# Shift products of two heads in their own row quarters of the TensorE array

## The chip, the cores and the metric

The kernel runs on one core of one Trainium2 chip. The metric is the device time of one execution in microseconds; the median of three executions of the kernel before is 4314.11 us (4312.82 to 4318.57).

The engines of a core have their own in-order instruction streams and meet through semaphores. TensorE multiplies (the profile calls its matmuls PE and its weight loads PEld), VectorE is DVE, ScalarE is ACT, GpSimd is POOL, and SyncE, or SP, issues the DMA transfers.

## What is computed

A transformer block with attention and a feed-forward network side by side on the same normalised input, in float32. The input has 8 sequences of 1024 tokens with 512 features; there are 16 heads of 32 features, and the network is 1408 wide.

```python
xn = _layernorm(x, axis=-1)
x = x + attention(xn) + ffn(xn)

# attention
qkv = xn @ W_attn + b_attn                     # q, k, v: 16 heads of 32
att = einsum('bhqd,bhkd->bhqk', q, k) * 32 ** -0.5
att = where(causal, att, -inf)
att = softmax(att, axis=-1)
y = einsum('bhqk,bhkd->bhqd', att, v)          # heads joined again
y @ W_proj + b_proj

# ffn: fp4_linear quantises and dequantises both operands in blocks of 16
h = silu(fp4_linear(xn, w_gate)) * fp4_linear(xn, w_up)
fp4_linear(h, w_down)
```

## The kernel before

**Streams.** One Python generator writes each kind of work: the projections to q, k and v (`prepare`, L464 and L509), the row maxima and sums of the scores (`maxima`, L594 to L608), the attention itself (`weigh`), the network (`network`, L793 and L815), its quantisation, and the output projection (`finish`, L920). `merge` interleaves them by hand into one program order. It keeps a planned clock: each `yield` names the TensorE cost of what was just issued, the time before which the next step should not begin, and how many banks that step wants. Actions for the other engines are put on a list with due times (`Later`) and come into the program when the planned clock passes them. So a cost in a `yield` does no work on the chip; it decides the order in which the streams are put.

**Banks.** Six PSUM banks of 128 x 512 (`Banks`) are shared by all streams. `take` hands out the one that should be free first, `back` returns it with the time at which its last reader should be done. Two more banks hold `y` and `acc`.

**A unit** is two heads (HU = 2) of one sequence; there are 64 units, eight for each sequence. A softmax here takes two passes. `maxima` finds each query's maximum, which is turned and kept in DRAM as a shift, split into a rounded part and a remainder. `weigh` then computes the scores again with keys on the partitions and queries along the columns, lays the shift onto them, and takes the exponential.

**The shift product.** `shT` is a 128 x 512 tile in F32R that is zero but for the first two rows of each quarter of 32 rows: quarter k = 2Q + r holds the two parts of the shift of head r for the half Q of the queries. `pick` holds four 128 x 128 matrices; the k-th is one in the rows of quarter k and zero elsewhere. The product of `pick[:, k, :]` with `shT` therefore adds up quarter k's rows, and puts the same sum on all 128 output partitions. It opens the accumulation in a bank; the score product (L713, keys as weights, queries as moving operand) closes it.

**The loop of `weigh`.** For each half Q of 512 queries, `j` runs over the key tiles of 128 keys that the causal mask lets through: 4 for Q = 0, 8 for Q = 1. On the diagonal only the columns from `q0` on are computed, so blocks are 512, 384, 256 or 128 columns wide. A block does, for each of the two heads in turn: take a bank, shift product (L710), score product (L713), exponential on ScalarE (L721), and on the diagonal a triangular select on GpSimd (L727). Per unit that is 12 blocks, 24 shift products and 24 score products; over all units 768 blocks.

After every second block `weighted` multiplies four such results with the values (L692). These four products have 32 output rows each and are placed side by side in the columns of the array by `tile_position=(0, row)`; each is a float32 product of two instructions, so a group has eight. There are 384 groups. Everything else on TensorE uses the array undivided.

The shift and score products are F32R and take one instruction each. The projections, the network and the weighting are float32, and take two.

Of the kernel before, what the change touches and what calls it, by code (L numbers as in the profile page):

```python
# [27 lines left out]
def kernel(  # L28
# [35 lines left out]
    HD = D // HEADS  # L64
# [6 lines left out]
    HU = 2  # L71
# [3 lines left out]
    W = QG * P  # L75
# [38 lines left out]
    pick = const.tile([P, HPC, P], F32R, name="pick")  # L114
# [33 lines left out]
    def act(columns, after=0.0, function="other"):  # L148
        if function == "other":
            function = table[0]  # L150
        switch = TABLE if function != table[0] else 0.0
        table[0] = function
        return on("act", 0.17 + 0.00083 * columns + switch, after)
# [4 lines left out]
    def pool(us, after=0.0):  # L158
        return on("pool", us, after)
# [52 lines left out]
    banks = Banks()  # L212
# [320 lines left out]
    def load_half(un, h):  # L533
        f, r0 = un.u * HU // HPC, un.u * HU % HPC
        for name, pool, s, pieces, lst in (("qs", p5, 0, (0, 0, 1, 1), un.qs), ("ks", p6, 1, (0, 1, 0, 1), un.ks)):
            tl = pool.tile([P, HU, W], F32R, name=name)
            for g, piece in enumerate(pieces):
                nc.sync.dma_start(
                    out=tl.bitcast(F32)[g * HD : (g + 1) * HD],
                    in_=un.batch.qk[s, piece, f, r0 * HD : (r0 + HU) * HD, h * W : (h + 1) * W].rearrange(  # L540
                        "(r d) t -> d r t", d=HD
                    ),
                )
            lst.append(tl)

    def load_values(un):
        for h in range(2):
            v = p4.tile([P, QG, HU * HD], F32, name="vs")
            cols = slice(un.u * HU * HD, (un.u + 1) * HU * HD)
            nc.sync.dma_start(  # L550
                out=v, in_=un.batch.v[h * QG : (h + 1) * QG, :, cols].rearrange("t p e -> p t e")
            )
            un.vs.append(v)
# [114 lines left out]
    def weigh(un):  # L668
        f, r0 = un.u * HU // HPC, un.u * HU % HPC
        emptied = 0.0  # L670
        while un.shT is None:
            yield 0.0, clock[0] + 0.5, 0
        units_begun[0] = un.n

        def loads(Q):
            if un.n + 2 < N:
                load_half(units[un.n + 2], Q)
            if un.n + 1 < N and Q == 0:
                load_values(units[un.n + 1])

        yield 0.0, un.ready, 2

        for Q in range(2):
            Later(1.0, lambda Q=Q: loads(Q))
            y = ps_a.tile([P, W], F32, name="y")
            last = (Q + 1) * QG - 1
            waiting = []
            def weighted():
                for j, r, pr, q0 in waiting:
                    h, jj = j // QG, j % QG  # L690
                    row = (j % 2 * HU + r) * HD
                    nc.tensor.matmul(  # L692
                        y[row : row + HD, q0:],
                        lhsT=un.vs[h][:, jj, r * HD : (r + 1) * HD],
                        rhs=pr[:, q0:],
                        start=(j < 2),
                        stop=(j >= last - 1),
                        skip_group_check=True,
                        tile_position=(0, row),
                    )  # L700
                return 0.3 + (W - min(q0 for _, _, _, q0 in waiting)) * 0.0017

            ready = 0.0
            for j in range(last + 1):
                h, jj = j // QG, j % QG
                q0 = jj * P if h == Q else 0
                fresh = []
                for r in range(HU):
                    bank, w = banks.take()
                    nc.tensor.matmul(  # L710
                        w[:, q0:], lhsT=pick[:, Q * HU + r, :], rhs=un.shT[:, q0:], start=True, stop=False
                    )
                    nc.tensor.matmul(  # L713
                        w[:, q0:],
                        lhsT=un.ks[h][:, r, jj * P : (jj + 1) * P],
                        rhs=un.qs[Q][:, r, q0:],
                        start=False,
                        stop=True,
                    )
                    pr = p8.tile([P, W], F32, name="pr")  # L720
                    nc.scalar.activation(pr[:, q0:], w[:, q0:], AF.Exp)  # L721
                    cost = max(0.22, (W - q0) * 0.00089)
                    end = act(W - q0, clock[0] + cost * (r + 1), "exp")
                    banks.back(bank, end)
                    if h == Q:

                        nc.gpsimd.affine_select(  # L727
                            out=pr[:, q0 : q0 + P],
                            in_=pr[:, q0 : q0 + P],
                            compare_op=ALU.is_ge,  # L730
                            fill=0.0,
                            base=0,
                            pattern=[[1, P]],
                            channel_multiplier=-1,
                        )
                        end = pool(0.37, end)
                    if j == 1 and q0 > 0:

                        nc.gpsimd.memset(pr[:, :q0], 0.0)
                        end = pool(0.2)  # L740
                    fresh.append((j, r, pr, 0 if j < 2 else q0))
                if j % 2 == 0 and waiting:
                    yield 2 * cost, max(ready, emptied), 0
                    yield weighted(), 0.0, 2
                    waiting = []
                else:
                    yield 2 * cost, 0.0, 2 if j < last else 0
                waiting += fresh
                ready = end
            yield 0.0, max(ready, emptied), 0  # L750
            cost = weighted()
            yu = p1.tile([P, W], F32, name="yu")
            nc.scalar.copy(yu, y)
            emptied = act(W, clock[0] + cost)

            def store(Q=Q, yu=yu):
                rows = slice(r0 * HD, (r0 + HU) * HD)
                for part in range(2):
                    nc.sync.dma_start(
                        out=un.batch.y[part, f, rows, Q * W : (Q + 1) * W],  # L760
                        in_=yu[part * HU * HD : (part + 1) * HU * HD, :],
                    )
                un.batch.units_done += Q

            Later(emptied - clock[0] + 0.5, store)
            yield cost, 0.0, 2
# [275 lines left out]
    with tc.manual_schedule(  # L1042
# [10 lines left out]
        for k in range(2 * NC):  # L1053
            w = p8.tile([P, NC, P], F32, name="pr")
# [9 lines left out]
        for col in range(2 * D, 3 * D, 2 * P):  # L1064
            w = p2.tile([P, NC, 2 * P], F32, name="wa")
# [48 lines left out]
        def preparations():  # L1114
            for n in range(AHEAD, N, QT):
# [3 lines left out]
        merge(  # L1119
            [  # L1120
                Stream((weigh(un), 17.5, un.n, 1.0) for un in units),
                Stream((maxima(un), 6.0, un.n - 1 - SOONER, 1.0) for un in units[1:]),
                Stream(networks()),
# [43 lines left out]
```

## Time and profile before

| | |
|---|---|
| median of three executions | 4314.11 us |
| the profiled execution | 4316.67 us |
| its span, first to last instruction | 4315.0 us |
| mean granted TensorE clock | 0.99 |
| shift products, L710 | 1536, 643.7 us busy, 427 ns on average |
| score products, L713 | 1536, 519.4 us busy, 346 ns on average |
| weighting, L692 | 3072 instructions, 358.1 us busy, 509 ns on average |
| exponential, L721 | 1536, 666.9 us busy, 494 ns on average |
| start of the first and of the last shift product | 295.4 and 4192.1 us |

A group's busy time is the time in which at least one of its instructions ran. A matmul's duration goes from its start to the end of its last result, and successive matmuls overlap; so durations add up to more than the span, and what a matmul costs the engine is the distance to the start of the next. Weight loads run in a row of their own beside the matmuls.

### The profile page before, as it was taken

The page shows a single profiled execution, that of the slowest core. Times are in us where ns is not written, and L with a number is a line of the kernel's source. Part 1 is how long each engine was busy: PE and PEld are TensorE (multiplying, and loading weights), DVE is VectorE, ACT ScalarE, POOL GpSimd, SP SyncE. Part 2 cuts the span into 40 slices and gives each one's busy share as a digit, 9 for nine tenths or more (in the row PEclk, how much of TensorE's full clock was granted, in tenths as well). Part 3 has the DMA queues.
Part 4 walks back from the last instruction along what each step waited for, and adds up shares of the span by engine and source line. Part 5 has one row for each costly group of instructions (what it writes and reads, how often), then busy time and mean ns, then how long its engine had stood idle before and what let it go on. Part 6 is the DMA issues. An engine that isn't in the chain of part 4 may idle for free.

```text
span 4315.0 us, 58501 instructions
## 1 busy us (share of the span) xinstructions
PE 4186.5 (97%) x17684; PEld 2574.7 (60%) x17684; DVE 2946.8 (68%) x6811; ACT 2331.1 (54%) x5918; POOL 551.6 (13%) x1295
## 2 busy tenths in 40 slices
PE   7779999999999999999999999999999999999998
PEld 6655556566666666666666666666666555555555
DVE  6786666666666766666766666766666677777755
ACT  2246565655555555555555555555555566666640
POOL 0001111111111111111111111111111111111110
PEclk9889999999999999999999999999999999999999
DMA  5654343454545554555554555554554433433424
GB/s 183 176 165 118 106 118 111 125 153 139 148 141 144 153 159 139 149 140 145 152 159 137 150 140 143 154 160 135 152 138 125 120 84 91 102 85 94 103 57 124
DMA packets 564185, 573.83 MB, mean 133 GB/s; under 512 B 114976, under 2 KB 420128, under 8 KB 563872
## 3 DMA queue, kind: packets, MB, share of 16 engines
q1 hardware_dynamic: 563872, 570.10, 47.8%
q8 instruction: 142, 2.33, 0.2%
q14 instruction: 171, 1.40, 0.1%
HBM read 400.56 MB, written 169.35 MB: 132 GB/s over the span
## 4 chain that ended last, share of the span: by engine, by line
PE 83%; DMA 3%; ACT 2%; DVE 2%; issue 1%; SPq 1%; ACTq 0%; POOL 0%; DVEq 0%
PE bank L815 26%; PE acc L793 13%; PE y L692 7%; PE bank L464 7%; PE bank L710 7%; PE bank L713 6%; PE bank L594 5%; PE bank L920 5%; PE bank L509 4%; PE bank L349 2%; ACT bank L566 2%; DVE neg L608 1%; DMA yT<-y_kept 1%; DMA ks<-y_kept 1%; DMA vs<-v_kept 0%
## 5 line engine op out<-in xcount | busy, mean ns | idle before, releaser
L608 DVE TENSOR_REDUCE neg<-bank 128x1 f32<-128x512 f32 (+3 forms) x1280 | 805.6, 635 | 292.3 <-PE bank L594 265.7
L721 ACT ACTIVATE pr<-bank 128x512 f32<-128x512 f32 (+3 forms) x1536 | 666.9, 494 | 517.5 <-PE bank L713 508.5
L566 ACT ACTIVATE bank<-bank,neg 128x512 f32<-128x512 f32 (+3 forms) x1536 | 857.9, 560 | 113.5 <-DVE neg L608 101.5
L727 POOL TENSOR_SCALAR_AFFINE_SELECT pr<-pr 128x128 f32<-128x128 f32 x1024 | 395.3, 397 | 3145.9 <-ACT pr L721 3139.2
L815 PE MATMUL bank<-wuT,xqT 128*128 128x512 f32 (+1 forms) x1536 | 674.7, 564 | 9.0 <-ACT bank L566 6.5
L815 PE MATMUL bank<-wgT,xqT 128*128 128x512 f32 (+1 forms) x1536 | 671.5, 561 | 0.0
L793 PE MATMUL acc<-wdT,hqT 128*128 128x512 f32 x1408 | 662.9, 595 | 1.3 <-ACT hqT L350 1.3
L594 PE MATMUL bank<-ks,qs 128*128 128x512 f32 (+3 forms) x1536 | 631.1, 469 | 20.1 <-ACT bank L566 14.5
L710 PE MATMUL bank<-shT,pick 128*128 128x512 f32 (+3 forms) x1536 | 643.7, 427 | 5.2 <-DMA shT<-shift_kept 3.6
L713 PE MATMUL bank<-qs,ks 128*128 128x512 f32 (+3 forms) x1536 | 519.4, 346 | 0.0
L606 DVE TENSOR_TENSOR bank<-bank,mask 128x128 f32<-128x128 f32 (+1 forms) x768 | 259.5, 338 | 342.6 <-PE bank L594 253.8
L594 PEld LDWEIGHTS bank<-ks,qs 128*128 128x128 f32 x1536 | 273.2, 191 | 266.4 <-issue 132.6
L476 ACT ACTIVATE full<-bank,bqk 128x256 f32<-128x256 f32 x256 | 107.5, 471 | 572.0 <-PE bank L464 503.6
L710 PEld LDWEIGHTS bank<-shT,pick 128*128 128x128 f32 x1536 | 290.8, 189 | 201.0 <-issue 94.1
L815 PEld LDWEIGHTS bank<-wuT,xqT 128*128 128x128 f32 x1536 | 273.8, 190 | 218.3 <-issue 140.6
L815 PEld LDWEIGHTS bank<-wgT,xqT 128*128 128x128 f32 x1536 | 276.0, 190 | 213.0 <-issue 164.8
L793 PEld LDWEIGHTS acc<-wdT,hqT 128*128 128x128 f32 x1408 | 258.3, 190 | 224.4 <-issue 204.1
L692 PE MATMUL y<-pr,vs 128*32 128x512 f32 (+3 forms) x3072 | 358.1, 509 | 4.7 <-POOL pr L727 4.6
L464 PE MATMUL bank<-xnT,wa 128*128 128x256 f32 x1536 | 352.2, 383 | 0.5 <-ACT xnT L350 0.5
L713 PEld LDWEIGHTS bank<-qs,ks 128*128 128x128 f32 x1536 | 291.2, 190 | 84.4 <-issue 51.9
L464 PEld LDWEIGHTS bank<-xnT,wa 128*128 128x128 f32 x1536 | 292.2, 192 | 64.8 <-issue 27.5
L566 ACT ACTIVATION_READ_ACCUMULATOR bank<-bank,neg 128x1 f32 x1536 | 316.0, 206 | 0.0
(97 smaller groups left out, 4501.5 us busy)
## 6 DMA issues: line engine op xcount, KB each, us to landing
wa<-in_L_attn_W_attn_dram SPq DMA_DIRECT2D x146, 512.0 KB
qs<-qk_kept SPq DMA_DIRECT2D x512, 128.0 KB
ks<-qk_kept SPq DMA_DIRECT2D x512, 128.0 KB
wp<-in_L_attn_W_proj_dram SPq DMA_DIRECT2D x81, 512.0 KB
qk_kept<-high SPq DMA_DIRECT2D x128, 256.0 KB
qk_kept<-full SPq DMA_DIRECT2D x128, 256.0 KB
y_kept<-yu SPq DMA_DIRECT2D x256, 128.0 KB
yT<-y_kept SPq DMA_DIRECT2D x112, 256.0 KB
```

The lines of the kernel that those rows point to most:

```text
L464: nc.tensor.matmul(pq[:, j, :], lhsT=halves[j][:, c, :], rhs=xnT[:, c, :], start=(c == 0), stop=(c == NC - 1),)
L566: nc.scalar.activation(part, part, AF.Exp, bias=neg[:, kind, k + j : k + j + 1], accum_out=sums[:, kind, k + j : k + j + 1],)
L594: nc.tensor.matmul(sc[:, j * n : (j + 1) * n], lhsT=un.qs[Q][:, r, i * P : (i + 1) * P], rhs=un.ks[h][:, r, :n], start=True, stop=True,)
L606: nc.vector.tensor_tensor(corner, corner, mask.unsqueeze(1).broadcast_to([P, count, P]), ALU.add)
L608: nc.vector.tensor_reduce(neg[:, kind, k : k + count], each, AX.X, ALU.max, negate=True)
L692: nc.tensor.matmul(y[row : row + HD, q0:], lhsT=un.vs[h][:, jj, r * HD : (r + 1) * HD], rhs=pr[:, q0:], start=(j < 2), stop=(j >= last - 1 ...
L710: nc.tensor.matmul(w[:, q0:], lhsT=pick[:, Q * HU + r, :], rhs=un.shT[:, q0:], start=True, stop=False)
L713: nc.tensor.matmul(w[:, q0:], lhsT=un.ks[h][:, r, jj * P : (jj + 1) * P], rhs=un.qs[Q][:, r, q0:], start=False, stop=True,)
L721: nc.scalar.activation(pr[:, q0:], w[:, q0:], AF.Exp)
L727: nc.gpsimd.affine_select(out=pr[:, q0 : q0 + P], in_=pr[:, q0 : q0 + P], compare_op=ALU.is_ge, fill=0.0, base=0, pattern=[[1, P]], channe ...
L793: nc.tensor.matmul(tl.acc, lhsT=job.hqT[:, j, :], rhs=wdT[:, i, :], start=(i == 0), stop=(i == NI - 1))
L815: nc.tensor.matmul(job.g, lhsT=job.tl.xqT[:, c, :], rhs=wT[:, c, job.i0 : job.i0 + job.w], start=(c == 0), stop=(c == NC - 1),)
```

## The change

In each block both banks are taken first. Then both shift products are issued, then, for each head, the score product, the exponential and what follows. A shift product now uses only its own quarter: 32 rows of `pick`, 32 rows of `shT`, and the 32 rows of the array from k x 32 on, with all 128 output columns. What it adds up is the same, since the other rows of that `pick` are zero. The score products still use all 128 rows. The planned cost of one head is changed from max(0.22, 0.00089 n) to max(0.2, 0.05 + 0.00067 n) for n columns.

```diff
-                for r in range(HU):
-                    bank, w = banks.take()
+                held = [banks.take() for _ in range(HU)]
+                for r, (_, w) in enumerate(held):
+                    k = Q * HU + r
+                    quarter = slice(k * HD, (k + 1) * HD)
                     nc.tensor.matmul(
-                        w[:, q0:], lhsT=pick[:, Q * HU + r, :], rhs=un.shT[:, q0:], start=True, stop=False
+                        w[:, q0:],
+                        lhsT=pick[quarter, k, :],
+                        rhs=un.shT[quarter, q0:],
+                        start=True,
+                        stop=False,
+                        tile_position=(k * HD, 0),
                     )
+                for r, (bank, w) in enumerate(held):
                     nc.tensor.matmul(
                         w[:, q0:],
                         lhsT=un.ks[h][:, r, jj * P : (jj + 1) * P],
...
                     nc.scalar.activation(pr[:, q0:], w[:, q0:], AF.Exp)
-                    cost = max(0.22, (W - q0) * 0.00089)
+                    cost = max(0.2, 0.05 + (W - q0) * 0.00067)
                     end = act(W - q0, clock[0] + cost * (r + 1), "exp")
                     banks.back(bank, end)
```

## The prediction, made before the result was known

> **What bounds the kernel now.** I read the page's busy shares first, then the busy time by stretch, then the chain of work that ended last, and last the single instructions of TensorE around one block of attention.
>
> ```profile
> span 4315.0 us, 58501 instructions
> ## 1 busy us (share of the span) xinstructions
> PE 4186.5 (97%) x17684; PEld 2574.7 (60%) x17684; DVE 2946.8 (68%) x6811; ACT 2331.1 (54%) x5918; POOL 551.6 (13%) x1295
> ...
> ## 4 chain that ended last, share of the span: by engine, by line
> PE 83%; DMA 3%; ACT 2%; DVE 2%; issue 1%; SPq 1%; ACTq 0%; POOL 0%; DVEq 0%
> PE bank L815 26%; PE acc L793 13%; PE y L692 7%; PE bank L464 7%; PE bank L710 7%; PE bank L713 6%; PE bank L594 5%; PE bank L920 5%; PE bank L509 4%; PE bank L349 2%; ACT bank L566 2%; DVE neg L608 1%; DMA yT<-y_kept 1%; DMA ks<-y_kept 1%; DMA vs<-v_kept 0%
> ```
>
> TensorE is the bound: 97% busy, 83% of the chain, and by stretch 994.5, 993.7 and 991.4 us busy in the three stretches of 1000 us from 1000 to 4000 us. VectorE is busy 68 to 71% there, ScalarE 56 to 60%. So a nanosecond that TensorE gains or loses in a block of attention is nearly a nanosecond of the span. The edited product is L710, 7% of the chain (about 300 us); its partner, the score product L713, has 6%.
>
> The groups with shapes kept apart give the counts (name, form, count, then busy us, mean ns and idle before):
>
> ```profile
> L710 PE MATMUL bank<-shT,pick 128*128 128x512 f32 x768 | 365.8, 476 | 4.6 <-DMA shT<-shift_kept 3.6 <-ACT bank L566 0.8 <-ACT full L476 0.2
> L710 PE MATMUL bank<-shT,pick 128*128 128x384 f32 x256 | 120.4, 470 | 0.3 <-ACT bank L566 0.3
> L710 PE MATMUL bank<-shT,pick 128*128 128x256 f32 x256 | 93.0, 385 | 0.1
> L710 PE MATMUL bank<-shT,pick 128*128 128x128 f32 x256 | 64.4, 277 | 0.2
> ```
>
> The means hold latency that overlaps the next product. What a product costs is the distance to the next start: from a score product to the following shift product the trace has a median of 231 ns at 512 columns, 174 at 384, 118 at 256 and 112 at 128 (the last is held by the weight load, not by the columns).
>
> **The key row: what a change of tiling costs here.** No product is tiled by rows before, but L692 is tiled by columns (four products of 32 columns side by side), so the trace shows what going into and out of a tiled form costs. First the timeline of TensorE's matmuls around one such group, then of its weight loads (start us, duration us, engine, line):
>
> ```profile
> 2017.35 0.39 PE L710 MATMUL bank<-shT,pick 128*128 128x512 f32 x1
> 2017.58 0.40 PE L713 MATMUL bank<-qs,ks 128*128 128x512 f32 x1
> 2017.91 1.06 PE L692 MATMUL y<-pr,vs 128*32 128x512 f32 x8
> 2018.90 0.50 PE L710 MATMUL bank<-shT,pick 128*128 128x512 f32 x1
> 2019.24 0.40 PE L713 MATMUL bank<-qs,ks 128*128 128x512 f32 x1
> ```
> ```profile
> 2017.36 0.19 PEld L713 LDWEIGHTS bank<-qs,ks 128*128 128x128 f32 x1
> 2017.91 0.16 PEld L692 LDWEIGHTS y<-pr,vs 128*32 128x32 f32 x8 [0.36 <-PE bank L713]
> 2018.90 0.19 PEld L710 LDWEIGHTS bank<-shT,pick 128*128 128x128 f32 x1 [0.84 <-issue]
> 2019.01 0.19 PEld L713 LDWEIGHTS bank<-qs,ks 128*128 128x128 f32 x1
> ```
>
> Three things are to be seen. Between full products the weights of the next load while the last one streams (2017.36, under the product of 2017.35). At the border they do not: the load of L692 starts at 2017.91, 0.33 us after the product of 2017.58 began, which streams for 0.23. Over the 384 groups of L692 this is steady: 522 ns from a 512-column f32 product (429 ns in a row of its own kind) to the group, 309 from a 256-column one (216), and out again 522 and 309. So **93 ns of drain in each direction**. Last, the load then has nothing to hide behind. The first L710 after the group lasts 0.50 instead of 0.39, and 0.34 us pass to the next start instead of 0.23. Loads of 32 columns take a median of 109 ns and of 128 columns 188, so 79 ns for 96 columns, about 0.83 ns each: **107 ns exposed for 128 columns**. Into a tiled form with loads of 128 columns and out again, that makes 93+107+93+107 = 400 ns. Inside, the tiled instructions start 7 ns apart (the eight loads of the fence fit in 0.16 us).
>
> **The change, part by part.**
>
> *Removed:* of each block's two shift products one disappears under the other. There are 768 blocks: 384 of 512 columns, 128 each of 384, 256 and 128. 384 x 0.231 + 128 x (0.174 + 0.118 + 0.112) = 88.7 + 51.7 = **140.4 us**. The two products name different rows, different weights and different banks, and L692 shows four column tiles really side by side (four two-instruction products in 0.99 us, where one alone needs 0.86).
>
> *Added:* each block now goes from the full array to row quarters and back, ahead of L713. The trace has no row tiling. Its bounds: below, no drain and hidden loads (7 ns for the second start); above, L692's price, 407 ns with that start. I take the upper end, the nearest row. 768 x 0.407 = **312.6 us**. Two corrections follow. At 128 columns the shift product behind its exposed load streams in 56 ns instead of the load-held 112: -7.2 us. And 121 of the 384 groups of L692 are followed directly by L710: their exit is paid already, and a change from column tiles to row tiles costs one border, not two: 121 x 0.200 = -24.2 us. Sum: 312.6 - 140.4 - 7.2 - 24.2 = **+140.8 us**.
>
> *A rule weighed.* The Trainium skill, "TensorE: Matmul & The Clock Gate", Part 3, gives tiles in one pack a span of one matmul plus about 4 ns for each further tile; by it alone each block drops a product, and the sum is about -137 us. But that describes the inside of a pack. The same skill's "TensorEngine Tiling (Array Packing)", Key Properties, says that changing the tiling mode, as against the tile, drains TensorE. The 93 ns above is that drain seen here for columns; that it is as large for rows no run here shows yet. The first page also says a load of 32 rows by 128 columns takes as long as one of 128 by 128, which is why I put 107 ns, not a quarter, at the entry. A pack of two products is small against two borders: **break-even is 140.4/768 = 183 ns a block**, less than one full border of 200 ns.
>
> *Moved:* both banks are taken ahead of the first product, so the second head's bank is wanted one score product (about 0.23 us) earlier. A block is only begun when the plan sees two banks free, and L710 has 5.2 us of idle ahead of it on TensorE in all: nothing. The two score products now end 0.23 us apart instead of 0.46, while an exponential (L721) takes 0.49 on average; the second head's waits behind the first's, some 0.2 us. The weighted product that needs it is held back by one further block, and its waits on ScalarE and GpSimd are about 36 us in all: nothing again. With that cover gone it would be up to 0.2 us in each of 384 groups, 77 us.
>
> *The plan's cost* for a pair falls from 0.911 to 0.786 us at 512 columns, so the hand-made order will think TensorE further on than it is. This changes which stream goes next and no work. Every instruction and DMA stays; SP's queue keeps its transfers, at slightly other places.
>
> *How much reaches the end.* TensorE has 20 us idle in the 3000 us from 1000 to 4000, but the chain also has 2% ScalarE and 2% VectorE, mostly banks not yet free from L566 and L608; slower blocks give those engines more time. I let a tenth of the 140.8 be absorbed: +127. Against the profiled execution's 4316.67 us (span 4315.0 and 1.67 around it) this is 4444; that execution lies 2.6 above the median 4314.11, so **4441 us** on the median's footing, own range 4395 to 4490.
>
> **Rivals.**
>
> *Row quarters drain little (faster).* Place: the two borders of each block. If a quarter's weights load behind the running full product and only one drain is left, the price is 100 ns: 768 x (0.100 - 0.183) = -64, 4250 us. With nothing left it is 4314 - 135 = about 4180. It decides from under 183 ns a block. For it: the weights of a row tile enter only their own rows, and full products do preload. Against it: L692's weights also have columns of their own and still waited, in every group.
>
> *One border is free (slightly slower or same).* One direction costs 200, the other nothing, or both drain with hidden loads (186): 768 x (0.193 to 0.207 - 0.183) = +8 to +18 us, 4322 to 4332; between this and the forecast lie shorter drains. For it: a 32-row product may leave the array earlier than a 128-row one. Against: L692 shows the same 93 in both directions.
>
> *The quarters do not run side by side.* Then nothing is removed and both borders stay: 141 + 140 = about +280, 4590 us. For it: each streams 128 columns of output into its own bank, which L692's tiles do not. Little else speaks for it.
>
> **How the numbers follow.** Forecast 0.60; one border free or shorter drains, up to 4395, 0.14; faster 0.20, of which 0.08 lies above 4250; not side by side 0.06. The range 4250 to 4500 leaves out 0.12 below, 0.06 above. About 0.2% (9 us) is what a measurement can tell from no change: faster 0.20, same 0.05, slower 0.75.
>
> **What would show it.** In the changed trace: the two L710 of a block start about 7 ns apart, with loads under no product; L710 after a 512-column f32 product starts 522 ns after it, not 429; the first L713 of a block starts about 93 ns later than its predecessor's streaming ends and lasts about 0.50, not 0.40; the second keeps 0.40. If L710's loads begin under the product before, the entry is free and I am wrong there; if L713's first load lies under L710, the exit is. If the two L710 start a product's length apart, the pack does not work.

## The result, and the profile after

The changed kernel takes 4453.69 us (median of four runs, 4449.51 to 4456.17) against 4314.2 us: 1.0319 times as long, 95% interval 1.0302 to 1.0335 (the two medians alone give 1.0323). That is **139.5 us slower**. The forecast was 4441 us, slower, with 4395 to 4490 as its own range. A slower result was right, and so was its cause; three terms of the sum were off and partly offset each other.

The page of the changed kernel, in the parts shown for the kernel before (L712 is now the shift product, L721 the score product, L729 the exponential, L801 and L823 the network):

```profile
span 4454.5 us, 58656 instructions
## 1 busy us (share of the span) xinstructions
PE 4329.3 (97%) x17684; PEld 2439.8 (55%) x17684; DVE 2948.9 (66%) x6811; ACT 2326.0 (52%) x5918; POOL 566.4 (13%) x1295
...
## 4 chain that ended last, share of the span: by engine, by line
PE 88%; ACT 2%; DVE 1%; DMA 1%; issue 1%; SPq 0%; ACTq 0%; POOL 0%; DVEq 0%
PE bank L823 28%; PE acc L801 13%; PE bank L721 9%; PE y L692 7%; PE bank L464 7%; PE bank L712 6%; PE bank L594 6%; PE bank L928 4%; PE bank L509 4%; PE bank L349 3%; ACT bank L566 1%; DMA qs<-inv_kept 0%; DVE neg L608 0%; ACT full L520 0%; ACT pr L729 0%
```

The count of matmuls is the same, VectorE and ScalarE are as busy as before, and TensorE has taken up the whole difference: 4329.3 us against 4186.5. The busy time of the shift products falls, as it should when two run at once (643.7 to 347.8 us). Yet the path hardly gains there (7 to 6%), and the score products on it grow from 6 to 9%, although nothing in them was edited. They carry the way back to the undivided array.

Two blocks of 512 columns in the changed trace, first the timeline of the matmuls and then that of the weight loads (start us, duration us, engine, line):

```profile
2008.95 0.63 PE L692 MATMUL y<-pr,vs 128*32 128x256 f32 x8
2009.50 0.50 PE L712 MATMUL bank<-shT,pick 32*128 32x512 f32 x2
2009.93 0.72 PE L721 MATMUL bank<-qs,ks 128*128 128x512 f32 x2
2010.49 0.40 PE L594 MATMUL bank<-ks,qs 128*128 128x512 f32 x1
2010.82 0.50 PE L712 MATMUL bank<-shT,pick 32*128 32x512 f32 x2
2011.25 0.73 PE L721 MATMUL bank<-qs,ks 128*128 128x512 f32 x2
```
```profile
2009.50 0.18 PEld L712 LDWEIGHTS bank<-shT,pick 32*128 32x128 f32 x2 [0.40 <-issue]
2009.93 0.30 PEld L721 LDWEIGHTS bank<-qs,ks 128*128 128x128 f32 x2 [0.24 <-issue]
2010.27 0.19 PEld L594 LDWEIGHTS bank<-ks,qs 128*128 128x128 f32 x1
2010.82 0.18 PEld L712 LDWEIGHTS bank<-shT,pick 32*128 32x128 f32 x2 [0.36 <-DVE high L489]
```

The two shift products are one row of 0.50 us, so they do lie side by side. From the full product at 2010.49 to the pair it is 0.33 us, where 0.23 would be streaming; the load at 2010.82 starts with its product and not ahead of it, unlike the load of L594 at 2010.27, which lies under the score product. From the pair to the first score product it is 0.43 us, which is 107 ns of load, 0.23 of streaming and 93 ns of drain.

Medians of the distances between starts over the 768 blocks of the changed trace. The row of the drain is 522 less 429 ns, and the step to an undivided product is put at its value before, since it differs by at most 2 ns:

| | 512 columns | 384 | 256 | 128 |
|---|---|---|---|---|
| first to second shift product | 3 ns | 3 | 3 | 3 |
| second shift product to first score product | 427 | 368 | 310 | 253 |
| first to second score product | 337 | 280 | 223 | 163.5 |
| second score product to an undivided product | 231 | 174 | 118 | 112 |
| drain at the entry | 93 | 93 | 93 | 93 |
| sum | 1091 | 918 | 747 | 624.5 |
| four products before | 924 | 696 | 472 | 448 |
| **more** | **167** | **222** | **275** | **176.5** |

With 384 blocks of the first width and 128 of each other that is 64.1 + 86.2 = 150.3 us. In the new order 165 weighting groups, not 121, are followed directly by shift products, and each such place saves one border of 0.2 us (its exit is paid already by the group): 150.3 - 33.0 = **117.3 us**. The other 22 of the 139.5 us are not borders. The experiments were made to find them, and to test the price of a border where it was not fitted.

### The profile page after: what moved, and what is told of

Same layout as the page of the kernel before. It is cut to its first block, busy times and chain, and to the rows that moved or that the text cites. A ratio compares the mean times of both kernels' runs of the same rounds, so it can differ in the third digit from the quotient of the medians.

```text
span 4454.5 us, 58656 instructions
## 1 busy us (share of the span) xinstructions
PE 4329.3 (97%) x17684; PEld 2439.8 (55%) x17684; DVE 2948.9 (66%) x6811; ACT 2326.0 (52%) x5918; POOL 566.4 (13%) x1295
## 4 chain that ended last, share of the span: by engine, by line
PE 88%; ACT 2%; DVE 1%; DMA 1%; issue 1%; SPq 0%; ACTq 0%; POOL 0%; DVEq 0%
PE bank L823 28%; PE acc L801 13%; PE bank L721 9%; PE y L692 7%; PE bank L464 7%; PE bank L712 6%; PE bank L594 6%; PE bank L928 4%; PE bank L509 4%; PE bank L349 3%; ACT bank L566 1%; DMA qs<-inv_kept 0%; DVE neg L608 0%; ACT full L520 0%; ACT pr L729 0%
## 5 line engine op out<-in xcount | busy, mean ns | idle before, releaser
L729 ACT ACTIVATE pr<-bank 128x512 f32<-128x512 f32 (+3 forms) x1536 | 664.4, 490 | 722.2 <-PE bank L721 711.4
L735 POOL TENSOR_SCALAR_AFFINE_SELECT pr<-pr 128x128 f32<-128x128 f32 x1024 | 406.4, 407 | 3322.5 <-ACT pr L729 3312.4
L823 PE MATMUL bank<-wuT,xqT 128*128 128x512 f32 (+1 forms) x1536 | 684.4, 570 | 10.7 <-ACT bank L566 5.2
L823 PE MATMUL bank<-wgT,xqT 128*128 128x512 f32 (+1 forms) x1536 | 672.5, 562 | 0.0
L801 PE MATMUL acc<-wdT,hqT 128*128 128x512 f32 x1408 | 668.4, 599 | 1.3 <-ACT hqT L350 1.3
L594 PE MATMUL bank<-ks,qs 128*128 128x512 f32 (+3 forms) x1536 | 630.2, 472 | 20.9 <-ACT bank L566 18.2
L721 PE MATMUL bank<-qs,ks 128*128 128x512 f32 (+3 forms) x1536 | 483.6, 396 | 0.0
L823 PEld LDWEIGHTS bank<-wuT,xqT 128*128 128x128 f32 x1536 | 277.2, 191 | 259.5 <-issue 180.4
L594 PEld LDWEIGHTS bank<-ks,qs 128*128 128x128 f32 x1536 | 274.8, 191 | 238.3 <-issue 125.0
L823 PEld LDWEIGHTS bank<-wgT,xqT 128*128 128x128 f32 x1536 | 275.1, 190 | 213.0 <-issue 139.0
L801 PEld LDWEIGHTS acc<-wdT,hqT 128*128 128x128 f32 x1408 | 255.3, 190 | 230.4 <-issue 218.1
L712 PEld LDWEIGHTS bank<-shT,pick 32*128 32x128 f32 x1536 | 145.2, 182 | 420.3 <-issue 221.4
L692 PE MATMUL y<-pr,vs 128*32 128x512 f32 (+3 forms) x3072 | 359.1, 511 | 4.0 <-POOL pr L735 3.9
L712 PE MATMUL bank<-shT,pick 32*128 32x512 f32 (+3 forms) x1536 | 347.8, 439 | 2.3 <-ACT xqT L350 1.7
L721 PEld LDWEIGHTS bank<-qs,ks 128*128 128x128 f32 x1536 | 229.8, 189 | 144.7 <-issue 119.0
```

The lines of the kernel that those rows point to most:

```text
L594: nc.tensor.matmul(sc[:, j * n : (j + 1) * n], lhsT=un.qs[Q][:, r, i * P : (i + 1) * P], rhs=un.ks[h][:, r, :n], start=True, stop=True,)
L692: nc.tensor.matmul(y[row : row + HD, q0:], lhsT=un.vs[h][:, jj, r * HD : (r + 1) * HD], rhs=pr[:, q0:], start=(j < 2), stop=(j >= last - 1 ...
L712: nc.tensor.matmul(w[:, q0:], lhsT=pick[quarter, k, :], rhs=un.shT[quarter, q0:], start=True, stop=False, tile_position=(k * HD, 0),)
L721: nc.tensor.matmul(w[:, q0:], lhsT=un.ks[h][:, r, jj * P : (jj + 1) * P], rhs=un.qs[Q][:, r, q0:], start=False, stop=True,)
L735: nc.gpsimd.affine_select(out=pr[:, q0 : q0 + P], in_=pr[:, q0 : q0 + P], compare_op=ALU.is_ge, fill=0.0, base=0, pattern=[[1, P]], channe ...
L801: nc.tensor.matmul(tl.acc, lhsT=job.hqT[:, j, :], rhs=wdT[:, i, :], start=(i == 0), stop=(i == NI - 1))
```

## The experiments

All are compared with the kernel before on the same chip.

| run | median us | against before, us | ratio, 95% interval |
|---|---|---|---|
| e1_plan_only | 4323.60 | +6.7 | 1.0015, 1.0008 to 1.0023 |
| e2_old_cost | 4445.92 | +129.0 | 1.0298, 1.0282 to 1.0313 |
| e3_true_cost | 4452.88 | +135.9 | 1.0313, 1.0297 to 1.0328 |
| e4_order_only | 4320.15 | +3.2 | 1.0005, 0.9997 to 1.0014 |
| e5_one_by_one | 4872.11 | +557.1 | 1.1290, 1.1274 to 1.1307 |
| e6_pack_of_four | 4365.90 | +50.9 | 1.0117, 1.0102 to 1.0132 |
| e7_shift_in_score | 4184.69 | -130.3 | 0.9697, 0.9680 to 0.9713 |
| e8_total_17 | 4170.31 | -144.1 | 0.9668, 0.9651 to 0.9684 |
| e9_total_10 | 4133.09 | -181.4 | 0.9579, 0.9565 to 0.9594 |

### The plan alone, and the tiling under other plans

e1 is the kernel before with the new planned cost:

```diff
-                    cost = max(0.22, (W - q0) * 0.00089)
+                    cost = max(0.2, 0.05 + (W - q0) * 0.00067)
```

> The kernel before, with the new planned cost alone: no row tiling, shift and score products in the old order within a block. Theory A (the borders of the row tiling are the whole loss): within 10 us of before, 4304 to 4324 us. Theory B (the plan's clock, which runs ahead of TensorE, costs about 20 us by worse interleaving): 4330 to 4340 us.

It is 6.7 us slower (3.5 to 10 by the interval), just inside A's window and below B's: by itself the plan costs little, but not nothing.

e2 is the changed kernel with the line with the minus, and e3 the changed kernel with

```diff
-                    cost = max(0.2, 0.05 + (W - q0) * 0.00067)
+                    cost = max(0.31, 0.2 + (W - q0) * 0.00067)
```

> The changed kernel with the old planned cost. From the changed trace, a block costs 167, 222, 275 and 177 ns more at 512, 384, 256 and 128 columns, 150 us over all blocks, less 0.2 us for each weighting group that is followed directly by shift products. Theory A: 4425 to 4455 us, like the changed kernel within 15 us. Theory B: some 20 us under the changed kernel, 4430 to 4436 us.

> The changed kernel with a planned cost that fits what its trace shows (0.2 us + 0.00067 us a column for one head, at least 0.31). Theory A: within 15 us of the changed kernel's 4454. Theory B: the loss over the bare border sum (117 us) goes, 4430 to 4436 us.

Both windows of e2 hold its 4445.9; e3 is in A's and not in B's. But the traces say more than the times, because the plan also decides how often a weighting group and a pair of shift products share a border. The steps of a block are the same to 1 ns in the traces of e2 and e3, so the border sum can be made for each:

| | shared borders | 150.3 less 0.2 each | measured | left over |
|---|---|---|---|---|
| changed kernel | 165 | 117.3 | 139.5 | 22 |
| e2, old planned cost | 121 | 126.1 | 129.0 | 3 |
| e3, planned cost as measured | 73 | 135.7 | 135.9 | 0 |

The intervals of the ratios make each left-over uncertain by about 7 us. So the rest of 22 us goes with the new planned cost, the one that runs furthest ahead of TensorE. B had the size right. It missed e3 because the truthful plan puts 92 fewer groups beside shift products and so pays 18 us more in borders. Of the 22, e1 shows 7 without any tiling; the other 15 appear only with tiling and this plan together.

In the middle of the kernel, where the order repeats from unit to unit, borders alone fit. Between the 384th and the 960th score product a unit takes 64.78 us before and 66.82 in e2: +2.04, where 150.3/64 less 1.5 shared borders of 0.2 is 2.05. The changed kernel takes 66.53 there, +1.74, and its border sum, with 2.5 shared borders a unit, is 1.85. So its 22 us lie outside the middle, and most of them ahead of it: at the 384th score product it is 47.5 us behind the kernel before, where borders make 29.6 (16 units of 2.35, less 40 shared borders). In that stretch its clock is lower. The clock rows of the two pages, in 40 slices of the span and in tenths, and the granted clock over the whole span, each first before and then changed:

```profile
PEclk9889999999999999999999999999999999999999
PEclk9888999999999999999999999999999999999999
core 0: 4315.0 us, clock 0.990
core 0: 4454.5 us, clock 0.986
```

One less the granted share, times the span, is the clock lost: 43 us before, 62 in the changed kernel, 56 in e1, 53 in e2 and in e3. In none of the five is any lost between the 384th and the 960th score product. The 19 us more of the changed kernel have about the size and the place of what is left over, so the new plan seems to cost time through the clock. No run shows that as the cause; e2 and e3 also lose 10 us of clock more than the kernel before, with next to nothing left over.

### The order alone

e4 issues both shift products and then both score products, all on the undivided array and with the old planned cost (cut from its difference to the changed kernel):

```diff
                     nc.tensor.matmul(
                         w[:, q0:],
-                        lhsT=pick[quarter, k, :],
-                        rhs=un.shT[quarter, q0:],
+                        lhsT=pick[:, k, :],
+                        rhs=un.shT[:, q0:],
                         start=True,
                         stop=False,
-                        tile_position=(k * HD, 0),
                     )
```

> Both shift products first and then both score products, as in the changed kernel, but all on the undivided array and with the old planned cost. Theory A (order costs nothing): 4309 to 4319 us, score and shift products 231 ns apart as before. Theory C (the two exponentials of a block come too close together, and the second bank is wanted too early): slower by up to 77 us, up to 4390 us.

The ratio 1.0005 has 1 in its interval. Taking both banks first, and two exponentials 0.23 us apart instead of 0.46, costs nothing that can be measured. The median is 1 us past A's window, and far from C.

### Borders without a pack

e5 puts each score product right behind its own shift product, so nothing runs side by side and a block has two excursions. Against the changed kernel:

```diff
-                held = [banks.take() for _ in range(HU)]
-                for r, (_, w) in enumerate(held):
+                for r in range(HU):
+                    bank, w = banks.take()
                     k = Q * HU + r
                     quarter = slice(k * HD, (k + 1) * HD)
...
                         tile_position=(k * HD, 0),
                     )
-                for r, (bank, w) in enumerate(held):
                     nc.tensor.matmul(
```

> Each head's shift product in its quarter, but with its score product right behind it, so a block has two excursions and packs nothing; new planned cost. Theory A (each border 93 ns of drain and 107 ns of exposed load, whatever is inside): +0.800 us a block, +0.63 at 128 columns, less what weighting groups share: about +560 us, 4860 to 4900 us. Theory D (the price belongs to the pack of two and not to the borders): only the pack's gain of 140 us is lost against the changed kernel, about 4590 us.

4872 us: inside A's window, and 280 us over D's. The timeline of one block:

```profile
2005.01 0.49 PE L712 MATMUL bank<-shT,pick 32*128 32x512 f32 x1
2005.43 0.49 PE L720 MATMUL bank<-qs,ks 128*128 128x512 f32 x1
2005.86 0.50 PE L712 MATMUL bank<-shT,pick 32*128 32x512 f32 x1
2006.28 0.50 PE L720 MATMUL bank<-qs,ks 128*128 128x512 f32 x1
2006.62 0.63 PE L594 MATMUL bank<-ks,qs 128*128 128x512 f32 x2
```

Every step between quarter and whole array takes 0.42 to 0.43 us, whichever way it goes, and the last, to another undivided product, only 0.34: no border, but still its own load of 107 ns. With the medians of all blocks (1.715 us a block, against 0.924, at 512 columns) the sum is +577 less the 33 for shared borders, 544 us. Against e1, which has the same plan, e5 takes 550 us more. In these two kernels a border has its price whatever lies between two of them, the same for one product as for two.

### A larger pack

Four shift products fill four quarters, two blocks at a time. `pick` becomes one tile of ones, and the shift rows of a half are loaded into quarters 0 and 1 and again into 2 and 3.

```diff
-            for j in range(last + 1):
+            for j0 in range(0, last + 1, 2):
+                spent = weighted() if waiting else 0.0
...
+                for c in range(2):
+                    for r in range(HU):
+                        bank, w = banks.take()
+                        k = c * HU + r
+                        quarter = slice(k * HD, (k + 1) * HD)
+                        nc.tensor.matmul(
+                            w[:, q0:],
+                            lhsT=pick[quarter, :],
+                            rhs=un.shT[Q][quarter, q0:],
+                            start=True,
+                            stop=False,
+                            tile_position=(k * HD, 0),
+                        )
```

> Two blocks at a time: their four shift products in all four quarters (the shift rows are loaded twice), right behind the weighting group of the two blocks before, then four score products. Four of the six banks are taken at once. Theory A: products removed 207 us (0.693 us for a pair of 512 columns, 0.579 for 512 and 384, 0.342 for 256 and 128); borders added 384 x 0.209 + 128 x 0.200 = 106 us; so about -100 us, 4213 us. Theory E (a pack waits for four free banks, and for the exponentials ahead of the weighting): not faster than before, 4314 us or more, with TensorE idle ahead of the packs.

4366 us: in time E is right, and A's forecast is off by 153 us. In the pack itself A is right. From the first start of a pack of four to the score products the median is 433 ns at 512 columns, against 430 for two, and 328 of the 384 packs follow a weighting group directly. So the borders and products alone would give -207 + 384 x 0.2 + 56 x 0.2 = -119 us. Two packs from the timeline show where it goes:

```profile
2003.27 0.39 PE L713 MATMUL bank<-shT,pick 32*128 32x256 f32 x4
2003.58 0.68 PE L726 MATMUL bank<-qs,ks 128*128 128x256 f32 x4
...
1418.19 0.38 PE L713 MATMUL bank<-shT,pick 32*128 32x256 f32 x3
1418.87 0.32 PE L713 MATMUL bank<-shT,pick 32*128 32x128 f32 x1 [0.30 <-ACT bank L564]
1419.12 0.68 PE L726 MATMUL bank<-qs,ks 128*128 128x256 f32 x4
```

The first pack runs in 0.31 us. The second stands with three quarters at work until ScalarE has read the fourth's bank, and takes 0.93. The mean pack is 565 ns at 512 columns and 391 at 256, so waits inside packs cost 256 x 0.132 + 128 x 0.078 = 44 us. TensorE's gaps between 1000 and 3000 us rise from 12 to 40 us, and its clock is granted for 0.981 of the span instead of 0.990, which is 40 us of clock lost more. These figures overlap in part, and how the 170 us between -119 and +51 are made up of them and of other waits was not taken apart.

### No shift products at all

The score product stacks four products of 32 rows: high times high, high times low, low times high, low times low. e7 leaves out the last, in the maxima as well as here, and puts the two shift rows against rows of ones in its place. No bank, load or matmul is left of the shift product. So e7 computes slightly less than the other kernels. Its planned costs were changed too: 0.000445 us a column for one head, at least 0.11, and 13.0 instead of 17.5 us for a unit's attention.

```diff
-        for name, pool, s, pieces, lst in (("qs", p5, 0, (0, 0, 1, 1), un.qs), ("ks", p6, 1, (0, 1, 0, 1), un.ks)):
+        for name, pool, s, pieces, lst in (("qs", p5, 0, (0, 0, 1), un.qs), ("ks", p6, 1, (0, 1, 0), un.ks)):
...
+            nc.sync.dma_start(out=tl.bitcast(F32)[3 * HD :], in_=fill[s])
             lst.append(tl)
...
-                    nc.sync.dma_start(out=un.shT.bitcast(F32)[row : row + 2, :], in_=un.shift[:, q, r, :])
+                    nc.sync.dma_start(out=un.qs[q].bitcast(F32)[row : row + 2, r, :], in_=un.shift[:, q, r, :])
...
-                    nc.tensor.matmul(
-                        w[:, q0:], lhsT=pick[:, Q * HU + r, :], rhs=un.shT[:, q0:], start=True, stop=False
-                    )
```

Here `fill` holds zeros for `qs`, and for `ks` two rows of ones over zeros.

> No shift products at all: the fourth quarter of the score product, which held low part times low part, holds the two rows of the shift against ones instead; the product of the two low parts is left out of scores and maxima. Theory A (TensorE is the bound, and the shift products' spacing is their price): all 1536 go, 2 x 140 = 281 us, about 4035 us. Theory F (VectorE, ScalarE or the banks take over): less than half arrives, over 4174 us.

130 of 281 us arrive; 4184.7 is F's side of the line, though TensorE is still 96% busy. The timeline of TensorE shows a place that returns every two units, and in just this form every four:

```profile
1200.59 0.44 PE L590 MATMUL bank<-ks,qs 128*128 128x384 f32 x1 [0.24 <-ACT bank L562]
1201.26 0.50 PE L590 MATMUL bank<-ks,qs 128*128 128x512 f32 x1 [0.23 <-ACT bank L562]
1202.39 0.51 PE L590 MATMUL bank<-ks,qs 128*128 128x512 f32 x1 [0.64 <-ACT bank L562]
1203.06 0.50 PE L590 MATMUL bank<-ks,qs 128*128 128x512 f32 x1 [0.16 <-ACT bank L562]
1203.73 0.50 PE L590 MATMUL bank<-ks,qs 128*128 128x512 f32 x1 [0.17 <-ACT bank L562]
1204.29 5.41 PE L504 MATMUL bank<-wa,xnT 128*128 128x256 f32 x16
```

A run of maxima (L590) waits at each step for a bank that ScalarE still has to read. Behind it the projection's sixteen products take 5.41 us, where the timeline of the kernel before has 3.61 for the same sixteen: the clock record has half speed for 3.4 us there. That pointed at the order, so e8 and e9 change one number of e7's plan:

```diff
-                Stream((weigh(un), 13.0, un.n, 1.0) for un in units),
+                Stream((weigh(un), 10.5, un.n, 1.0) for un in units),
```

(17.5 in e8.)

> The kernel without shift products, with one number of the plan changed: the planned total of a unit's attention 17.5, as before the change, where the first version had 13.0 (its real sum is some 10.5). Theory G (the missing 150 of 281 us lie in the interleaving: bursts of maxima wait for banks that ScalarE has yet to free, and the clock is halved for 3.4 us behind such a burst): the time moves by more than 10 us against 4185, and the clock time lost moves with it. Theory F (ScalarE and VectorE cannot go faster): within 10 us of 4185, whatever the order.

> The same with 10.5, so that a unit's attention is spread over the whole of its period. Theory G: moved by more than 10 us against 4185, faster if the maxima come in smaller bursts, with a granted clock over 0.976. Theory F: within 10 us of 4185.

The time moves by 14 and by 52 us, and the clock lost, one less the granted share times the span, goes from 100 to 75 and 54 us. So F, by which no order helps, falls, and of G the part on the clock stands. The waits hardly move with the time: those of the maxima for banks make 44, 48 and 39 us in e7, e8 and e9, and TensorE's idle time (span less busy time) is 173, 173 and 171. It is the busy time that falls, by 17 and 51 us. Since 17.5 and 10.5 both beat 13.0, the runs give no rule for the number. From the page of e9:

```profile
span 4129.7 us, 55463 instructions
## 1 busy us (share of the span) xinstructions
PE 3959.2 (96%) x16148; PEld 2334.4 (57%) x16148; DVE 2952.5 (71%) x6808; ACT 2310.3 (56%) x5918; POOL 528.5 (13%) x1292
...
PE 81%; ACT 7%; DVE 3%; DMA 2%; issue 2%; SPq 1%; POOL 0%; ACTq 0%; DVEq 0%; POOLq 0%
```

e9, at **4133 us, beats both kernels** by 4.2% and 7.2%. It still misses 100 us of the 281. TensorE's idle time is 42 us more than before, and ScalarE has 7% of the chain against 2%, so waits for it have come up beside TensorE; the rest was not taken apart.

## Why the prediction was right, and where not

- **Drain.** The step took 93 ns in each direction from the column tiles of L692. For row quarters it is 93 too: 522 ns from a 512-column f32 product to the pair, as forecast. (That a shift product stood 429 behind such a product before was misread: its recorded start is 28 ns behind it, and its score product's another 633. The two steps together, 661, are 429 and 231, so the sum is not touched.) The rivals with a free or a cheap border fall, e5 most plainly.
- **Exposed loads.** 107 ns at entry and exit, from loads of 32 and 128 columns. The load of a quarter lasts as long as one of all rows (182 ns on average, against 189), and the first and second score product are 337 ns apart instead of 231. The Trainium skill says so of the load in "TensorE: Matmul & The Clock Gate", LDWEIGHTS, and of the drain in "TensorEngine Tiling (Array Packing)", Key Properties; here both hold, with numbers.
- **The pack works.** Second start after 3 ns (7 were taken); the rival of quarters that do not run side by side falls.
- **Mis-sized: the narrow blocks.** For 128 columns the working gave 407 - 112 - 56 = +239 ns; it is +176.5. The two score products were charged their load-held 112 each, but 163.5 ns are all there is from first to second, the first's load of 107 included. With 9 to 14 ns too much in the others, all blocks come to 150.3 us, not 165.0.
- **Mis-sized: shared borders.** 121 were counted in the old order; the new one has 165. 33 us are saved, not 24.
- **Wrong in sign: "I let a tenth of the 140.8 be absorbed".** Instead of -14 us there are +22 beyond the borders. The step saw banks not yet free as slack that slower blocks would fill, and held that the plan "changes which stream goes next and no work". Gaps between TensorE's products from 1000 to 3000 us only fall from 12 to 7 us, and in e1, without slower blocks, they fall to 7 as well; so there was little to absorb, and no sign that slower blocks absorbed it. The plan's cost shows in the left-over table above; how it comes about stays open but for the clock.
- **Banks and exponentials** at nothing: right, by e4.
- **Slips without effect.** VectorE was 67 to 71% busy by stretch, not 68 to 71, and 79 ns for 96 columns are 0.82 ns each.

Borders too high by 24 us and the rest too low by 36 gave 127 for 139.5. The mechanism was right; the near agreement of the total is partly luck.

## What to carry to other kernels

Count borders, not products: here a change of the TensorE's tiling costs a drain and a weight load with no cover, 0.2 us each way, so two F32R products of up to 0.23 us do not pay for a pack. Four would by the sum of their borders (-119 us), but the run that tried it was 51 us slower, with packs that waited for banks. Here a trace that had one kind of tiling priced another well enough to decide before building. And a product whose use is two rows was better given rows in a product that runs anyway, where rows could be freed for it.

## What was not expected of the hardware

The clock was halved behind stretches in which TensorE was not idle but thin: in e7 five maxima products in 3.7 us, with waits of 0.16 to 0.64 us, were followed by 3.4 us at half speed, and each of the nine such places between 1079 and 2077 us has such 3.4 us at or just behind its end. It is a cost that comes after the wait and lands on other work: 1.8 us for the sixteen products shown. How thin a stretch must be was not measured. Nor can lost clock be read as lost time one to one: e5 lost some 30 us more of it than e1 and still fits its border sum to 6 us.
